# A two-layer graph network in float32: transposing the norms on VectorE with on-chip transfers instead of on TensorE, and the bound check's products made once

## The chip, the cores and the metric

The kernel runs on one core of a Trainium2 chip. A core has TensorE (matrix products and transposes, results in PSUM banks), VectorE, ScalarE, GpSimd and SyncE; SyncE (SP in the profile) issues the transfers, which 16 DMA engines carry out. Each engine works through its own queue in order and waits on semaphores for the others. The metric is the time of one execution in device microseconds, as a median over runs.

## The reference

x holds 64 graphs of 256 nodes with 512 features, adj one 256 x 256 adjacency matrix for all of them. Two layers follow one another; each normalizes x over its features, applies a relu and adds the result of an attention over the neighbours.

```python
def _L0_gnn_ref(X, A, W, a):
    h = jnp.einsum('bnf,fo->bno', X, W)                 # 512 -> 256
    e = h @ a[0] + jnp.swapaxes(h @ a[1], 1, 2)
    e = jax.nn.leaky_relu(e, 0.2) + NEG * (1.0 - A)[None]
    out = jnp.einsum('bij,bjo->bio', jax.nn.softmax(e, axis=-1), h)
    return jnp.concatenate([out, h], axis=-1)

def _L1_gnn_ref(h, adj, Wq, bq, Wk, bk, Wv, bv, Wo, bo):  # 8 heads of 64
    q, k, v = (split_heads(h @ W.T + b) for W, b in ((Wq, bq), (Wk, bk), (Wv, bv)))
    scores = jnp.einsum('bhqd,bhkd->bhqk', q, k) / 8.0
    scores = jnp.where((adj == 0)[None, None], -jnp.inf, scores)
    out = jnp.einsum('bhqk,bhkd->bhqd', jax.nn.softmax(scores, axis=-1), v)
    return out.transpose(0, 2, 1, 3).reshape(b, n, 512) @ Wo.T + bo

h = jnp.maximum(_layernorm(x), 0.0)
x = x + _L0_gnn_ref(h, adj, L0_gnn_W, L0_gnn_a)
h = jnp.maximum(_layernorm(x), 0.0)
x = x + _L1_gnn_ref(h, adj, Wq, bq, Wk, bk, Wv, bv, Wo, bo)
```

The norm of a tile has nodes on its 128 partitions and features along them. A product over the features needs the features on the partitions, so every tile of 128 nodes x 512 features is transposed in both layers.

## The kernel before

**Tiling.** A group is two graphs (`GB = 2`, called batches here), that is four tiles (`GT = 4`) of 128 nodes; there are 32 groups. Everything is float32.

**Stages of a group.** `first_layer(g)` (L396) computes the statistics (`stats`), normalizes and transposes each tile with `norm_T` (L343), multiplies by W (`ph`), forms the neighbour softmax (`pn`, `e`), applies it (`po`), takes the statistics of the new x, normalizes and transposes again into `hT1`, and has GpSimd form sums of quarter blocks of it (`operand_sums`, L374). `project(g)` (L483) makes q, k and v from these by a scheme of seven block products instead of eight (`pq`, `pk`, `pv`; a product numbered 1 to 4 can use a quarter as it stands or one weight sum, those numbered 3, 5, 6 and 7 need `sums`). `scores` (L553) multiplies q and k for four heads (`sc`), ScalarE takes exponentials into `p`, VectorE multiplies by the mask, GpSimd adds halves into `ps`. `weigh` (L581) multiplies by v (`pr`), adds up the denominators (`total`), and VectorE divides into `oT`. `outputs` (L611) makes the output products (`py`), again by seven, from `oT` and GpSimd's `o_sums`; VectorE adds each to x and SP stores it.

**The order.** The generators of three groups are interleaved by a string for each of four steps of an iteration: "u" advances `project(g + 1)`, "o" the outputs, "s" `first_layer(g + 2)`. An iteration ends with the last scores' follow-up, and the next begins with `sc` for group g + 1, at once followed by `pq` for group g + 2 and `py`. TensorE's order is kept as written by `in_order`; a scheduler places the other engines' work. Five PSUM banks go round under the tag `turn` (`mm`), three more are held.

**Norm and transpose.** `normed(t)` subtracts the mean and multiplies by the reciprocal deviation on VectorE into `xn` (two buffers). `put(t, dst)` transposes the four 128 x 128 pieces on TensorE against an identity matrix into a PSUM bank `pt` (L116), and ScalarE's relu takes the bank into `hT`:

```python
pt = mm(f"pt{name}_{t}").rearrange("p (c t) -> p c t", c=HP)
for c in range(HP):
    transpose(pt[:, c, :], xn[t][:, c * P : (c + 1) * P], ident)
nc.scalar.activation(dst, pt, AF.Relu)
```

**The bound check.** `judge()` (L224) bounds scores and values from the weights; if a bound fails, `any_inputs` recomputes everything in another way. It loads blocks of Wq, Wk and Wv again (L247, L267), forms Gram matrices per pair of heads (`gram`), squares them three times (`square`) and adds squares. It runs in places of the main loop where the first layer's generator yields a gap.

**SP's queue.** It holds the loads of x (one per group, L125, into four buffers), the weights' loads, the check's block loads, and one store for each batch (L654). Transfers share eight semaphores in turn, so one waits until the transfer eight places earlier has landed.

Of the kernel before, what the change touches and what calls it, by code (L numbers as in the profile page):

```python
# [8 lines left out]
F32 = mybir.dt.float32  # L9
# [5 lines left out]
P = 128  # L15
# [27 lines left out]
def bounded(  # L43
# [74 lines left out]
    xg = x.rearrange("(g b) (t p) d -> g p (b t) d", b=GB, p=P)  # L118
    og = out.rearrange("(g b) (t p) d -> g p (b t) d", b=GB, p=P)
# [3 lines left out]
    def load(g):  # L123
        xs[g] = big.tile([P, GT, D], F32, tag="x", name=f"x{g}", bufs=4)
        nc.sync.dma_start(xs[g], xg[g])  # L125

    load(0)


# [34 lines left out]

    load(1)
    load(2)


# [40 lines left out]
    def last_bias():  # L209


        pb = mm("pb")
        for q in range(NQ):
            for half in range(2):
                b = small.tile([P, P], F32, tag="power", name=f"bv_{q}_{half}", bufs=1)
                nc.vector.tensor_scalar(b, ones, bv_col[:, half, q : q + 1], None, op0=ALU.mult)
                matmul(
                    pb, b, w_sb["o"][:, half, 2 * q : 2 * q + 2, :],
                    start=(q == 0 and half == 0), stop=(q == NQ - 1 and half == 1),
                )  # L220
        nc.vector.tensor_add(b_out, pb, b_out)


    def judge():  # L224
# [6 lines left out]
        junk = att.tile([P, D], F32, tag="junk", name="junk", bufs=1)  # L231

        def squares(col, *srcs):
            sums = small.tile([P, HP], F32, tag="sums", name=f"sums{col}", bufs=2)
            for i, src in enumerate(srcs):
                nc.scalar.activation(
                    junk[:, : src.free_size()], src, AF.Square, accum_out=sums[:, i : i + 1]
                )
            nc.vector.reduce_sum(part[:, col : col + 1], sums[:, : len(srcs)], axis=AX.X)

        for s in range(2):
            squares(s, w0_sb[:, :, s])
        squares(2, *[w0_sb[:, c, 2:] for c in range(HP)])
        wv = att.tile([P, HP, D // HP], F32, tag="block", name="wv_block", bufs=1)
        sums = small.tile([P, HP], F32, tag="sums", name="sums3", bufs=2)
        for c in range(HP):
            nc.sync.dma_start(  # L247
                wv, wvT[:, c * P : (c + 1) * P].rearrange("(c p) o -> p c o", p=P)
            )
            nc.scalar.activation(  # L250
                junk, wv.rearrange("p c o -> p (c o)"), AF.Square, accum_out=sums[:, c : c + 1]
            )
        nc.vector.reduce_sum(part[:, 3:4], sums, axis=AX.X)
        squares(4, bcol["q"])
        squares(5, bcol["k"])
        squares(6, bv_col.rearrange("p h q -> p (h q)"))
        nc.vector.reduce_max(part[:, 7:8], bad.rearrange("p a t -> p (a t)"), axis=AX.X)
        yield
        heads = const.tile([P, P], F32, name="heads")
        nc.vector.memset(heads, 0.0)  # L260
        for j in range(2):
            nc.vector.memset(heads[j * DH : (j + 1) * DH, j * DH : (j + 1) * DH], 1.0)
        rowsq = const.tile([P, 2, HP], F32, name="rowsq")
        for n, (name, src) in enumerate((("q", wqT), ("k", wkT))):
            for hp in range(HP):
                w = att.tile([P, HP, P], F32, tag="block", name=f"w{name}_block{hp}", bufs=1)
                nc.sync.dma_start(  # L267
                    w, src[:, hp * P : (hp + 1) * P].rearrange("(c p) o -> p c o", p=P)
                )
                yield  # L270
                gram = mm(f"gram_{name}{hp}")[:, :P]
                for c in range(HP):
                    matmul(
                        gram, w[:, c, :], w[:, c, :], start=(c == 0), stop=(c == HP - 1)
                    )
                a = small.tile([P, P], F32, tag="power", name=f"power_{name}{hp}_0", bufs=1)
                nc.vector.tensor_mul(a, gram, heads)
                yield
                for i in range(3):
                    square = mm(f"square_{name}{hp}_{i}")[:, :P]  # L280
                    matmul(square, a, a, start=True, stop=True)
                    if i < 2:
                        a = small.tile(
                            [P, P], F32, tag="power", name=f"power_{name}{hp}_{i + 1}", bufs=1
                        )
                        nc.vector.tensor_copy(a, square)
                    else:
                        nc.scalar.activation(
                            junk[:, :P], square, AF.Square, accum_out=rowsq[:, n, hp : hp + 1]
                        )  # L290
                    yield
        nc.vector.reduce_sum(part[:, 8:10], rowsq, axis=AX.X)
# [45 lines left out]
    def stats(mv, src, t, name):  # L338
        st = small.tile([P, 6], F32, tag="st", name=f"st{name}_{t}")
        nc.vector.bn_stats(st, src[:, t, :])  # L340
        nc.vector.bn_aggr(mv[:, t, :], st)

    def norm_T(src, mv, name):  # L343
# [6 lines left out]
        xn = {}  # L350

        def normed(t):
            xn[t] = att.tile([P, D], F32, tag="xn", name=f"xn{name}_{t}", bufs=2)
            latest[0] = nc.vector.tensor_scalar(  # L354
                xn[t], src[:, t, :], mv[:, t, 0:1], rstd[:, t : t + 1],
                op0=ALU.subtract, op1=ALU.mult,
            ).ins.name

        def put(t, dst):
            if t + 1 < GT:  # L360
                normed(t + 1)
            pt = mm(f"pt{name}_{t}").rearrange("p (c t) -> p c t", c=HP)
            for c in range(HP):
# [710 lines left out]
```

## Time and profile before

| | us |
|---|---|
| three runs | 2698.94, 2701.87, 2702.36 |
| median | 2701.87 |
| the profiled execution | 2699.08 |
| its span, first to last instruction | 2697.3 |
| TensorE busy in that span | 2620.4 |
| VectorE busy | 1669.7 |
| GpSimd busy | 1230.0 |
| ScalarE busy | 835.9 |
| TensorE busy in the first 100 us | 68.4 |
| TensorE busy from 400 to 800 us | 397.3 |
| `pt` products (the transposes), 1024 | 156.2 |
| relu from `pt`, 256 | 153.1 |
| mean granted clock of TensorE | 0.993 |

A line of the profile gives the program's line, the engine, the operation, what is written from what, and the shape. In the groups there follow the total busy time, the mean duration in ns, and the idle time of the engine just before, with what ended it. In a timeline a line begins with the start and the duration in us; "x4" means four instructions one after another, and a number in brackets at the end is idle time before it with its releaser. TensorE's instructions overlap, so the cost of one in a stream is the distance of starts. In a table by stretches there stand, after the bounds and the length, the busy times of TensorE, its weight loads, VectorE, ScalarE and GpSimd, the granted clock, the DMA share and GB/s. "PEclk" in the page is the granted clock in tenths, over 40 slices. A line of the DMA issues ends with KB each and the median us from issue to landing.

### The profile page before, as it was taken

The page shows a single profiled execution, that of the slowest core. Times are in us where ns is not written, and L with a number is a line of the kernel's source. Part 1 is how long each engine was busy: PE and PEld are TensorE (multiplying, and loading weights), DVE is VectorE, ACT ScalarE, POOL GpSimd, SP SyncE. Part 2 cuts the span into 40 slices and gives each one's busy share as a digit, 9 for nine tenths or more (in the row PEclk, how much of TensorE's full clock was granted, in tenths as well). Part 3 has the DMA queues.
Part 4 walks back from the last instruction along what each step waited for, and adds up shares of the span by engine and source line. Part 5 has one row for each costly group of instructions (what it writes and reads, how often), then busy time and mean ns, then how long its engine had stood idle before and what let it go on. Part 6 is the DMA issues. An engine that isn't in the chain of part 4 may idle for free.

```text
span 2697.3 us, 41512 instructions
## 1 busy us (share of the span) xinstructions
PE 2620.4 (97%) x17150; PEld 2118.8 (79%) x17150; DVE 1669.7 (62%) x2558; ACT 835.9 (31%) x1771; POOL 1230.0 (46%) x1004
## 2 busy tenths in 40 slices
PE   5999999999999999999999999999999999999997
PEld 3888888878888887887788888788878878878874
DVE  5666566666557665566665576665576656666544
ACT  2333232333332333323333323333333333233321
POOL 2353355443445443545434454435455335445343
PEclk8999999999999999999999999999999999999998
DMA  5000101000001010000000000000000000000000
GB/s 164 1 12 32 36 24 36 13 32 32 28 32 36 9 36 32 24 32 9 32 32 24 32 32 9 32 32 24 32 32 9 32 32 24 32 17 23 17 16 25
DMA packets 45890, 78.49 MB, mean 29 GB/s; under 512 B 3712, under 2 KB 10624, under 8 KB 45696
## 3 DMA queue, kind: packets, MB, share of 16 engines
q1 hardware_dynamic: 45696, 75.77, 8.1%
q8 instruction: 137, 2.24, 0.3%
q14 instruction: 57, 0.47, 0.1%
HBM read 42.21 MB, written 33.55 MB: 28 GB/s over the span
## 4 chain that ended last, share of the span: by engine, by line
PE 89%; DVE 8%; POOL 1%; issue 1%; DMA 0%; ACT 0%; DVEq 0%
PE pq L113 15%; PE pv L113 14%; PE py L113 13%; PE pk L113 13%; PE pr L113 9%; PE ph L113 8%; PE sc L113 7%; PE po L113 4%; PE pt L116 4%; DVE p L573 3%; DVE r L604 2%; PE total L113 2%; DVE k L544 1%; DVE oT L605 1%; PE pn L116 1%
## 5 line engine op out<-in xcount | busy, mean ns | idle before, releaser
L573 DVE TENSOR_TENSOR p<-p,maskT 128x1024 f32<-128x1024 f32 x256 | 398.6, 1588 | 0.6 <-ACT p L572 0.5
L572 ACT ACTIVATE p<-sc 128x512 f32<-128x512 f32 x512 | 264.4, 602 | 380.9 <-PE sc L113 380.9
L574 POOL TENSOR_TENSOR ps<-p 128x512 f32<-128x512 f32 x256 | 366.2, 1447 | 0.0
L628 DVE TENSOR_TENSOR x<-py,x 128x256 f32<-128x256 f32 x448 | 187.6, 419 | 272.8 <-PE py L113 266.9
L604 DVE RECIPROCAL r<-total 128x256 f32<-128x256 f32 x128 | 224.5, 1754 | 194.6 <-PE total L113 194.6
L113 PE MATMUL py<-wo_sb,o_sums 128*128 128x256 f32 x1024 | 266.5, 384 | 26.4 <-DVE x L628 21.6
L420 POOL TENSOR_TENSOR x<-H,x 128x256 f32<-128x256 f32 x128 | 87.7, 685 | 443.0 <-ACT H L419 441.9
L113 PE MATMUL pr<-p,v 128*32 128x256 f32 x4096 | 251.8, 385 | 5.8 <-DVE p L573 5.8
L113 PE MATMUL sc<-q,k 64*128 64x256 f32 x2048 | 255.7, 389 | 0.0
L113 PE MATMUL pq<-sums,wq_sb 128*128 128x256 f32 x1024 | 246.7, 384 | 4.2 <-POOL sums L377 3.7
L113 PE MATMUL ph<-w_sb,hT 128*128 128x258 f32 x1024 | 246.1, 383 | 0.0
L113 PE MATMUL pk<-sums,wk_sb 128*128 128x256 f32 x1024 | 244.8, 382 | 0.0
L113 PE MATMUL pv<-wv_sb,sums 128*128 128x256 f32 x1024 | 242.0, 379 | 0.1
L113 PEld LDWEIGHTS sc<-q,k 64*128 64x128 f32 x2048 | 187.2, 186 | 69.7 <-issue 52.6
L113 PEld LDWEIGHTS py<-wo_sb,o_sums 128*128 128x128 f32 x1024 | 191.2, 192 | 62.9 <-POOL o_sums L377 37.6
L365 ACT ACTIVATE hT<-pt 128x512 f32<-128x512 f32 x256 | 153.1, 599 | 266.0 <-PE pt L116 265.7
L354 DVE TENSOR_SCALAR xn<-x,mv,rstd 128x512 f32<-128x512 f32 x256 | 225.8, 893 | 9.5 <-PE pt L116 4.9
L376 POOL TENSOR_TENSOR o_sums<-oT 128x256 f32<-128x256 f32 x64 | 106.2, 1660 | 262.6 <-DVE oT L605 262.6
L113 PEld LDWEIGHTS pq<-sums,wq_sb 128*128 128x128 f32 x1024 | 190.1, 191 | 39.1 <-issue 9.9
L113 PEld LDWEIGHTS ph<-w_sb,hT 128*128 128x128 f32 x1024 | 195.7, 192 | 28.6
L113 PEld LDWEIGHTS pk<-sums,wk_sb 128*128 128x128 f32 x1024 | 189.3, 190 | 33.9 <-issue 9.9
L113 PEld LDWEIGHTS pr<-p,v 128*32 128x32 f32 x4096 | 121.1, 110 | 112.2 <-issue 39.7
(145 smaller groups left out, 4054.4 us busy)
## 6 DMA issues: line engine op xcount, KB each, us to landing
x<-in_x_dram SPq DMA_DIRECT2D x32, 1024.0 KB, 5.5
out_dram<-x SPq DMA_DIRECT2D x64, 512.0 KB, 2.8
wq_sb<-in_L_gnn_Wq_dram SPq DMA_DIRECT2D x2, 512.0 KB, 11.7
wk_sb<-in_L_gnn_Wk_dram SPq DMA_DIRECT2D x2, 512.0 KB, 12.4
wv_sb<-in_L_gnn_Wv_dram SPq DMA_DIRECT2D x2, 512.0 KB, 11.4
wo_sb<-in_L_gnn_Wo_dram SPq DMA_DIRECT2D x8, 128.0 KB, 3.3
wv_block<-in_L_gnn_Wv_dram SPq DMA_DIRECT2D x4, 256.0 KB, 3.0
wq_block<-in_L_gnn_Wq_dram SPq DMA_DIRECT2D x4, 256.0 KB, 2.9
```

The costliest lines, as they stand in the source:

```text
L113: in_order(nc.tensor.matmul(*args, **kwargs))
L116: in_order(nc.tensor.transpose(*args))
L354: latest[0] = nc.vector.tensor_scalar(xn[t], src[:, t, :], mv[:, t, 0:1], rstd[:, t : t + 1], op0=ALU.subtract, op1=ALU.mult,).ins.name
L365: nc.scalar.activation(dst, pt, AF.Relu)
L376: nc.gpsimd.tensor_add(sums[:, 0], a21, a22)
L420: nc.gpsimd.tensor_add(xt[:, t, F1:], H[:, t, 2 : F1 + 2], xt[:, t, F1:])
L544: nc.vector.tensor_add(part(1, 1), first, p7)
L572: nc.scalar.activation(pair[:, j], sc[j], AF.Exp, scale=scale)
L573: nc.vector.tensor_mul(pair, pair, maskT[:, None, :, :].to_broadcast([P, 2, NT, N]))
L574: nc.gpsimd.tensor_add(ps[:, 2 * i : 2 * i + 2, :], pair[:, :, 0, :], pair[:, :, 1, :])
L604: nc.vector.reciprocal(r, total)
L628: nc.vector.tensor_add(to, out, to)
```

## The change

Except in group 0, a tile's norm is no longer transposed on TensorE. VectorE transposes it in 32 x 32 blocks into `xt`; 16 transfers per batch, each 32 partitions x 2 tiles with runs of 512 bytes, move the blocks between partition groups into `moved`; ScalarE's relu reads `moved` in the order that `hT` needs. The work of a batch is split: `norm` for its two tiles, `turn` (transposes and transfers), and later `placed` (the two relus), with a yield between them. The loads of x are one per batch (seven buffers). The check takes its products from the weights already on the chip, for all four pairs of heads of a matrix in one bank, and is advanced while group 0's first layer and projection run; its block loads are gone. `last_bias` makes its columns on GpSimd into one wide tile. The three `kept` tiles of `project` share one tag with two buffers.

```diff
-    def load(g):
-        xs[g] = big.tile([P, GT, D], F32, tag="x", name=f"x{g}", bufs=4)
-        nc.sync.dma_start(xs[g], xg[g])
+    def load(g, b):
+        xs[g, b] = big.tile([P, NT, D], F32, tag="x", name=f"x{g}_{b}", bufs=7)
+        nc.sync.dma_start(xs[g, b], xg[g, b])
...
+        b = att.tile([P, 2, 2, P], F32, tag="kept", name="bv_wide")
         for q in range(NQ):
             for half in range(2):
-                b = small.tile([P, P], F32, tag="power", name=f"bv_{q}_{half}", bufs=1)
-                nc.vector.tensor_scalar(b, ones, bv_col[:, half, q : q + 1], None, op0=ALU.mult)
+                nc.gpsimd.tensor_scalar(
+                    b[:, half, q, :], ones, bv_col[:, half, q : q + 1], None, op0=ALU.mult
+                )
...
+        for n, name in enumerate(("q", "k")):
+            gram = bank(f"gram_{name}")
+            for hp in range(HP):
+                half, cols = hp // 2, slice(hp % 2 * P, (hp % 2 + 1) * P)
+                for c in range(HP):
+                    w = w_sb[name][:, c % 2, c // 2 * 2 + half, cols]
+                    matmul(gram[:, hp, :], w, w, start=(c == 0), stop=(c == HP - 1))
+            power[name] = room[:, n * HP : (n + 1) * HP, :]
+            nc.vector.tensor_mul(
+                power[name], gram, heads[:, None, :].to_broadcast([P, HP, P])
+            )
+            yield
+        for i in range(3):
+            for n, name in enumerate(("q", "k")):
+                square = bank(f"square_{name}{i}")
+                for hp in range(HP):
+                    a = power[name][:, hp, :]
+                    matmul(square[:, hp, :], a, a, start=True, stop=True)
...
+                yield
...
-    def norm_T(src, mv, name):
+    def norm_T(src, mv, name, by_pe):
...
+        def turn(b):
+            tiles = range(b * NT, (b + 1) * NT)
+            if by_pe:
+                for t in tiles:
+                    turned[t] = mm(f"pt{name}_{t}").rearrange("p (c n) -> p c n", c=HP)
+                    for c in range(HP):
+                        transpose(turned[t][:, c, :], xn[t][:, c * P : (c + 1) * P], ident)
+                return
+
+            J = P // S
+            xt = att.tile([P, J, NT, P], F32, tag="xt", name=f"xt{name}_{b}")
+            moved = att.tile([P, NT, J, P], F32, tag="moved", name=f"moved{name}_{b}")
+            for t in tiles:
+                nc.vector.transpose(
+                    xt[:, :, t % NT, :].rearrange("p j (n c) -> p j c n", c=HP),
+                    xn[t].rearrange("p (c j a) -> p j c a", j=J, a=S),
+                )
+                turned[t] = moved[:, t % NT].rearrange("p i (n c) -> p c (i n)", c=HP)
+            for i in range(J):
+                for j in range(J):
+                    nc.sync.dma_start(
+                        moved[j * S : (j + 1) * S, :, i, :], xt[i * S : (i + 1) * S, j]
+                    )
+
         def put(t, dst):
...
+            nc.scalar.activation(dst, turned[t], AF.Relu)
...
-        put = norm_T(xt, mv, f"1_{g}")
+        norm, turn, put = norm_T(xt, mv, f"1_{g}", by_pe)
+        norm(0)
+        norm(1)
         yield GAP
         hT = big.tile([P, HP, TOK], F32, tag="hT1", name=f"hT1_{g}")
-        for t in range(GT):
-            put(t, hT[:, :, t * P : (t + 1) * P])
-            if t == GT - 1:
-                break
-            yield
+        ahead((turn, 0), (norm, 2), (norm, 3))
+        yield GAP
+        ahead((turn, 1))
+        yield GAP
+        placed(0, hT[:, :, :N])
+        yield GAP
+        placed(1, hT[:, :, N:])
...
-                s = att.tile([P, 2, N], F32, tag=f"kept{i}", name=f"kept{i}_{name}_{g}", bufs=1)
+                s = att.tile([P, 2, N], F32, tag="kept", name=f"kept{i}_{name}_{g}")
...
-    gaps = 0
-    for part in first_layer(0):
-        gaps += part is GAP
-        if part is GAP and gaps == 3:
+    verdict = judge()
+    for piece, _ in enumerate(first_layer(0)):
+        if piece == 8:
+            next(verdict)
+        if piece == 13:
             last_bias()
+            next(verdict)
+        if piece == 15:
             weight_sums("q")
     short = first_layer(1) if NG > 1 else none
     for i, _ in enumerate(project(0)):
-        if i % 7 == 1:
+        if i in (1, 8, 15):
             weight_sums("kvo"[i // 7])
         next(short, None)
+        next(verdict, None)
+    run(verdict)
     run(short)
-    verdict = judge()
...
-            if step == 1 and g + 3 < NG:
-                load(g + 3)
+            if step % 2 and g + 3 < NG:
+                load(g + 3, b)
...
-                elif next(short, GAP) is GAP:
-                    next(verdict, None)
+                else:
+                    next(short, None)
```

The first layer's norm is split in the same way, with `turn` and `placed` for each batch, before the `ph` products; the second batch's relus stand after the second `ph`. Elsewhere `xt[:, r, ...]` becomes a list of tiles `xt[r]` with the same operations.

## The prediction

> **What bounds the kernel now.** I read the busy shares first, then the costly groups, then the timeline of one iteration of the main loop, the DMA issues and the clock by stretches.
>
> ```profile
> PE 2620.4 (97%) x17150; PEld 2118.8 (79%) x17150; DVE 1669.7 (62%) x2558; ACT 835.9 (31%) x1771; POOL 1230.0 (46%) x1004
> ...
> PEclk8999999999999999999999999999999999999998
> ...
> L365 ACT ACTIVATE hT<-pt 128x512 f32<-128x512 f32 x256 | 153.1, 599 | 266.0 <-PE pt L116 265.7
> L354 DVE TENSOR_SCALAR xn<-x,mv,rstd 128x512 f32<-128x512 f32 x256 | 225.8, 893 | 9.5 <-PE pt L116 4.9
> ```
>
> TensorE is busy 97% at full clock, so what leaves it shortens the run, as long as nothing else becomes late. What a transpose costs on TensorE is read from starts, not from busy time:
>
> ```profile
> 1659.64 0.60 PE L116 MATMUL pt<-ident,xn 128*128 128x128 f32 x4
> 1659.84 0.59 ACT L514 COPY kept_v<-pv 128x512 f32<-128x512 f32 x1 [2.87 <-PE pv L113]
> 1659.97 1.60 PEld L113 LDWEIGHTS pv<-wv_sb,sums 128*128 128x128 f32 x8
> 1660.08 1.89 PE L113 MATMUL pv<-wv_sb,sums 128*128 128x256 f32 x8
> ```
>
> Four transposes start at 1659.64 and the next product at 1660.08; over several such places the step is 0.43 us a tile. In the same iteration GpSimd turns the transposed norms into operands:
>
> ```profile
> 1668.66 1.28 POOL L376 TENSOR_TENSOR sums<-hT 128x512 f32<-128x512 f32 x1 [1.22 <-PE pv L113]
> ...
> 1670.73 2.00 PE L113 MATMUL sc<-q,k 64*128 64x256 f32 x16
> ...
> 1675.50 1.59 POOL L377 TENSOR_TENSOR o_sums<-o_sums,oT 128x256 f32<-128x256 f32 x1
> ...
> 1677.95 1.03 PE L113 MATMUL py<-wo_sb,o_sums 128*128 128x256 f32 x4
> ```
>
> GpSimd's chain (three `sums`, the fourth, two `o_sums`) runs from 1668.66 to 1677.1, 8.4 us, and TensorE takes the result at 1677.95, 7.2 us after the scores (`sc`) begin. That chain has 0.85 us to spare today.
>
> **The change, part by part.**
>
> 1. *Transposes leave TensorE.* 31 of 32 groups x 8 tiles = 248 x 0.433 = 107.4 us off.
>
> 2. *The bound check leaves the main loop.* On the chain of waits one iteration's first scores stand at 191.31 and, twelve iterations on, at 1176.49: 82.10 us each. The next takes 86.58 (to 1263.07), later ones 81.55 (to 1344.62). The excess is 12 x 0.55 + 5.0 = 11.6 us; the products stand ahead of the loop instead, and 12 block loads (L247, L267) leave SP's queue.
>
> 3. *The start.* TensorE is busy 68.4 of the first 100 us. `pb` no longer passes through one buffer (its four steps lie between 45.40 and 52.8), and its columns are made by GpSimd: the first `pq` can start near 46.5 instead of 55.91, -9. The six squaring steps of four products add 6 x 0.87 = 5.2 between the products of `project(0)`. Group 1's own moves are exposed: its second layer has only seven `pv` products and one `sc` (14 us) over a path of about 31 us (the steps of part 4), some 17 us, of which the shorter products ahead give back a few. I take +5 for the whole start, with bounds of -9 and +20.
>
> 4. *The new path* is two block transposes on VectorE per batch (T each), 16 DMAs of 32 KB on SP's queue, and two relus on ScalarE. I follow it where it is tightest: the second layer of group g+2, at the end of an iteration. Zero is the start of its last `po` product (in the trace: 1649.17). TensorE then has `pk`, `py`, `pr`, `total`, `sc`, seven `pv`, `pr`, `total`, and reaches the next iteration's `sc` at +22.3 by its steps (1.73 a product, 0.87 a `py`, 1.75, 0.55, 1.93); the `py` that needs `o_sums` is due 7.2 later, at +29.5.
>    Supply: VectorE has the last statistics and `ve` at +3.9 (reciprocal starts 1.07 after `po`; 0.17, 0.48, 0.69 and the next group's first statistics in front), GpSimd's power takes 1.2, two `xn` unblocked 0.54 each: +6.2. T is not in the trace. At the same tile of 128x512 f32 the nearest rows are `xn` 0.54 and a tensor-tensor 0.69; the slowest VectorE row is the reciprocal, 1.75. I take 0.69: +7.6.
>    SP: the nearest rows have the same shape, 32 partitions x 2 runs, back to back:
>
> ```profile
> 24.57 0.42 SPq L187 DMA_DIRECT2D bv_col<-in_L_gnn_bv_dram  x1
> 25.04 0.43 SPq L186 DMA_DIRECT2D wo_sb<-in_L_gnn_Wo_dram  x1
> 25.51 0.42 SPq L187 DMA_DIRECT2D bv_col<-in_L_gnn_bv_dram  x1
> ...
> bv_col<-in_L_gnn_bv_dram SPq DMA_DIRECT2D x8, 0.2 KB, 2.4
> bq_sb<-in_L_gnn_bq_dram SPq DMA_DIRECT2D x1, 2.0 KB, 2.2
> ```
>
>    0.47 us from issue to issue and 2.3 to landing. Bounds: 0.31 (the isolated issues from 15.10 on) and 1.36 (their spacing while earlier transfers are waited for) for the one, 0.31 (no landing before the issue is over) and 5.5 (the 1 MB load) for the other. The first batch's 16, with the x load between them (0.5), hold SP to +15.6. The second batch's blocks are ready by then (a reciprocal 1.75, two `xn`, `oT` 0.69, two `p` products at 1.22, two T: +14.9; with mean durations +16.4). Its last DMA is issued at +22.65 and lands at +24.95; two relus, 1.2: +26.15; GpSimd's 8.4 us: +34.6. Due at +29.5, so TensorE stands still for 5.1 us.
>    Queued behind: ScalarE's relu waits for 16 DMAs, and the exponentials of the next scores stand behind it, then VectorE's `p` products and the `x` addition that empties the bank of `py`. That path comes to about +30.6, inside the same stall. On SP the next group's 32 DMAs follow; their `ph` is not due before about +43, and they land by +33.4 and +40.9. Stores and loads of x stand in the gaps between the bursts.
>    A stall of this length also lowers the clock:
>
> ```profile
> 104.00:108.00 4.00, 2.25 (x13) 2.00 (x14) 3.09 (x5) 0.80 (x2) 2.98 (x3) 1.00 0.00 0
> ...
> 1254.00:1258.00 4.00, 3.25 (x10) 2.79 (x11) 2.31 (x6) 0.60 (x1) 2.92 (x2) 0.57 0.00 0
> ...
> 1254.74 1.12 PE L116 MATMUL pt<-ident,xn 128*128 128x128 f32 x4 [2.92 <-DVE xn L354]
> 1255.65 2.95 PE L113 MATMUL pv<-wv_sb,hT 128*128 128x256 f32 x8
> ```
>
>    After 2.17 us of idleness at 105.75 the granted clock stays 1.00; after 2.92 us it is 0.57 in the next 4 us, the transposes take 0.91 instead of 0.43 and the product 2.79 instead of 1.73: +1.5.
>    So 5.1 + 1.5 = 6.6 us for each of the 30 iterations that prepare a later group: +198.
>    The loads of x by halves I put at nothing: they are issued 40 us and more ahead of use (without that cover, the 5.5 us to landing of a load). So too the three `kept` buffers that become two: the third product's copy waits for the first one's addition (0.68), which lies behind two products of 1.73; uncovered it would be 3 x 0.68 = 2 us an iteration.
>
> **Sum against the profiled execution.** 2697.3 - 107.4 - 11.6 + 5 = 2583.3 without stalls; + 198 = 2781.3 of span. That execution took 2699.08, 1.8 more than its span, and the median of the runs is 2.8 above it: 2786.
>
> **Two rules of the skill that speak against it.** T by the rows is 0.69. The Trainium skill ("VectorE: DVE Perf Modes", The three transpose paths) says that VectorE transposes only within 32x32 blocks and that a full 128x128 transpose belongs on TensorE. It gives 311 ns for a 128x128 bf16 tile; as an estimate from that page four make 1.24 us for T, the second batch's blocks would come at about +17.1, and the sum would be about 45 us higher. For the transfers the rows above give 0.47 us each, overlapped. The skill ("DMA: Bandwidth & Descriptors", Bandwidth) calls transfers under 64 KB dominated by their descriptors and lists 0.68 us at 4 KB and 0.95 at 64 KB; as an estimate from that page, 16 transfers of 0.8 one after another would take 12.8 us instead of 7.5, the second batch would land about 10 us later, and the sum would be about 300 us higher.
>
> **Rivals.**
> - *A, the forecast: the move path is too long by 5 us an iteration.* For it: the 8.4 us chain with 0.85 to spare, and 32 issues in a row on one queue. Against it: issue and landing between on-chip buffers are in no row.
> - *B, issues are quick.* At 0.31 us an issue the second batch starts with VectorE at +14.9 and lands at +21.85: a stall of 2.0 with no loss of clock, 60 us in all: 2583.3 + 60 + 4.6 = 2648. Faster. It decides below 3.8 us an iteration ((2697.3 - 2583.3) / 30), that is, when the second batch lands before about +23.7 (+22.2 with the loss of clock).
> - *C, all is hidden.* Landing by +19.9 needs issues under 0.2 us: 2583.3 + 4.6 = 2588. For it only that no row excludes it.
> - *D, VectorE is late too.* T of 1.4 and mean durations put the second batch's blocks at +19.2: a stall of 8.7 + 1.5, 306 us: 2894. For it: the four-dimensional patterns of the transpose and VectorE's share of 62%, which 248 x T raises; against it: the `xn` and tensor-tensor rows.
>
> **Chances.** A 0.62, B 0.15, C 0.10, D 0.08; 0.05 for an outcome so near 3.8 us an iteration that it is no change (within 0.2%, which is what a measurement of this kernel can tell). Faster 0.25, same 0.05, slower 0.70. A's own range is 2710 to 2855 (1.0 us either way in issues, landing and T moves the sum by 30). The range for 8 in 10 reaches down through B: 2620 to 2855.
>
> **What would show it.** In the new profile: `pt` groups only in group 0; an iteration of about 78.1 us plus the stall, 84 to 85 in all; TensorE waiting once an iteration at the `py` product for GpSimd's `o_sums`, which waits for the relu, which waits for the `moved` DMAs; granted clock of 0.5 to 0.7 just after; 16 DMAs at 0.47 us and T near 0.69; no check products after 115 us. Landings before +22, or issues of 0.3 us, would make the forecast wrong, and iterations near 78 us would show it.

## The result, and the profile after

The changed kernel takes 3034.62 us (median; 3032.71 to 3036.09) against 2700.94 us for the kernel before on the same chip: a ratio of 1.1236, 95% interval 1.1216 to 1.1255. The forecast was slower, 2786 us; it is slower by 334 us instead of 84, above the forecast's range of 2620 to 2855.

The page of the profile after, head, clock by slices, two groups and one transfer line:

```profile
PE 2664.0 (88%) x16158; PEld 2085.9 (69%) x16158; DVE 1829.0 (60%) x2783; ACT 950.7 (31%) x1759; POOL 1231.1 (41%) x1008
...
PEclk9899999999999999999999999999999999999998
...
L382 ACT ACTIVATE hT<-moved 128x512 f32<-128x512 f32 x248 | 266.6, 1125 | 349.9 <-DMA moved<-xt 349.7
...
L370 DVE STREAM_TRANSPOSE xt<-xn 128x512 f32<-128x512 f32 x248 | 257.5, 1095 | 39.0 <-DMA moved<-xt 39.0
...
moved<-xt SPq DMA_DIRECT2D x1984, 32.0 KB, 1.9
```

TensorE has 992 instructions fewer, which are the 248 x 4 transposes, yet it is busy for 2664 us instead of 2620 and idle for 367 instead of 77. Its mean granted clock is 0.941 instead of 0.993. The relu takes 1.125 us and the block transpose 1.095.

The waits of TensorE in the kernel after (us in total, times, longest):

```profile
PE py L113 <- POOL o_sums L389: 144.6, 31, 5.0
...
PE pv L113 <- ACT kept_v L551: 78.6, 30, 4.7
```

One end of an iteration in the kernel after, in the order of the new path (the timeline, start and duration in us). Its wait at `py` is one of the two shortest; most are near 5.0 us, as the list of waits says (144.6 us in 31 times):

```profile
1670.62 1.03 PE L113 MATMUL po<-H,e 128*128 128x257 f32 x4
...
1675.63 1.00 DVE L352 TENSOR_SCALAR xn<-x,mv,rstd 128x512 f32<-128x512 f32 x2 [0.74 <-POOL rstd L347]
...
1676.55 2.07 DVE L370 STREAM_TRANSPOSE xt<-xn 128x512 f32<-128x512 f32 x2
...
1678.68 2.18 SPq L377 DMA_DIRECT2D moved<-xt  x3
...
1680.96 0.53 SPq L125 DMA_DIRECT2D x<-in_x_dram  x1
...
1689.87 3.11 PE L113 MATMUL pv<-wv_sb,hT 128*128 128x256 f32 x8 [2.58 <-ACT kept_v L551]
...
1694.84 3.78 PE L113 MATMUL pv<-wv_sb,sums 128*128 128x256 f32 x8 [1.86 <-DVE v L581]
...
1701.70 2.14 ACT L382 ACTIVATE hT<-moved 128x512 f32<-128x512 f32 x2 [2.45 <-DMA moved<-xt]
...
1703.91 1.27 POOL L388 TENSOR_TENSOR sums<-hT 128x512 f32<-128x512 f32 x1 [12.59 <-ACT hT L382]
...
1711.49 0.72 POOL L389 TENSOR_TENSOR o_sums<-o_sums,oT 128x256 f32<-128x256 f32 x1
...
1712.26 1.13 PE L113 MATMUL py<-wo_sb,o_sums 128*128 128x256 f32 x4 [2.94 <-POOL o_sums L389]
```

From the start of the last `po` to the `py` that needs `o_sums` it is 41.64 us; the forecast had 34.6. SP's queue in the same stretch:

```profile
1681.54 39.61 SPq L377 DMA_DIRECT2D moved<-xt  x61
```

61 issues in a row without a gap, 0.65 us each. The first 32 (with the three before the load) are this group's second layer, the other 32 the next group's first layer.

Over the starts of `pv` of some twenty iterations (between 600 and 2410 us), the mean iteration of the kernel after is 91.98 us (81.96 before) and the mean distance from `po` to `py` 42.11 (29.17 before).

### The profile page after: what moved, and what is told of

Read it like the earlier page. It is cut to its first block, busy times and chain, and to the rows that moved or that the text cites. A ratio compares the mean times of both kernels' runs of the same rounds, so it can differ in the third digit from the quotient of the medians.

```text
span 3031.1 us, 42733 instructions
## 1 busy us (share of the span) xinstructions
PE 2664.0 (88%) x16158; PEld 2085.9 (69%) x16158; DVE 1829.0 (60%) x2783; ACT 950.7 (31%) x1759; POOL 1231.1 (41%) x1008
## 4 chain that ended last, share of the span: by engine, by line
PE 66%; POOL 9%; DVE 9%; SPq 8%; issue 3%; ACT 3%; DMA 3%; DVEq 0%; ACTq 0%; POOLq 0%
PE pk L113 13%; PE py L113 12%; PE pq L113 11%; SPq L377 7%; PE ph L113 7%; PE pr L113 7%; PE sc L113 7%; PE po L113 4%; PE pv L113 3%; DVE p L610 3%; POOL sums L389 2%; DVE xt L370 2%; POOL sums L390 2%; DMA moved<-xt 2%; PE total L113 2%
## 5 line engine op out<-in xcount | busy, mean ns | idle before, releaser
L610 DVE TENSOR_TENSOR p<-p,maskT 128x1024 f32<-128x1024 f32 x256 | 429.0, 1707 | 14.0 <-ACT p L609 13.8
L113 PE MATMUL py<-wo_sb,o_sums 128*128 128x256 f32 x1024 | 291.7, 417 | 148.0 <-POOL o_sums L389 144.6
L382 ACT ACTIVATE hT<-moved 128x512 f32<-128x512 f32 x248 | 266.6, 1125 | 349.9 <-DMA moved<-xt 349.7
L113 PE MATMUL pv<-wv_sb,hT 128*128 128x256 f32 x768 | 228.2, 458 | 78.6 <-ACT kept_v L551 78.6
L113 PE MATMUL pq<-sums,wq_sb 128*128 128x256 f32 x1024 | 284.3, 428 | 12.9 <-POOL sums L389 10.3
L370 DVE STREAM_TRANSPOSE xt<-xn 128x512 f32<-128x512 f32 x248 | 257.5, 1095 | 39.0 <-DMA moved<-xt 39.0
L113 PEld LDWEIGHTS pq<-sums,wq_sb 128*128 128x128 f32 x1024 | 222.8, 220 | 63.2 <-POOL sums L389 12.9
L113 PEld LDWEIGHTS pv<-wv_sb,sums 128*128 128x128 f32 x1024 | 196.3, 194 | 93.7 <-DVE v L581 67.2
L113 PEld LDWEIGHTS pv<-wv_sb,hT 128*128 128x128 f32 x768 | 167.9, 225 | 128.0 <-ACT kept_v L551 90.6
L113 PEld LDWEIGHTS sc<-q,k 64*128 64x128 f32 x2048 | 187.8, 187 | 70.6 <-issue 53.3
L507 POOL TENSOR_TENSOR x<-x,b_out 128x512 f32<-128x512 f32 x128 | 199.1, 1565 | 76.2 <-DVE xn L352 71.7
```

Source lines behind the costliest of these rows:

```text
L113: in_order(nc.tensor.matmul(*args, **kwargs))
L370: nc.vector.transpose(xt[:, :, t % NT, :].rearrange("p j (n c) -> p j c n", c=HP), xn[t].rearrange("p (c j a) -> p j c a", j=J, a=S),)
L382: nc.scalar.activation(dst, turned[t], AF.Relu)
L507: nc.gpsimd.tensor_add(xt[t], xt[t], b_out)
L610: nc.vector.tensor_mul(pair, pair, maskT[:, None, :, :].to_broadcast([P, 2, NT, N]))
```

## The experiments

Twelve kernels were run. "Path" is the mean distance from the last `po` to the first `py` that reads `o_sums`, "iteration" the mean distance of `pv` starts, both read from the timelines.

| run | us | ratio to before, 95% | iteration | path |
|---|---|---|---|---|
| all_pe | 2748.86 | 1.0187 (1.0170 to 1.0204) | 83.19 | 32.43 |
| layout | 2973.76 | 1.1017 (1.0998 to 1.1035) | 89.84 | 40.26 |
| four | 2839.52 | 1.0521 (1.0504 to 1.0539) | 86.36 | 38.65 |
| free_kept | 3000.08 | 1.1117 (1.1099 to 1.1136) | 90.58 | 41.94 |
| one_run | 2954.34 | 1.0936 (1.0917 to 1.0954) | 89.18 | 39.74 |
| two_q | 2806.10 | 1.0391 (1.0374 to 1.0408) | 84.59 | 36.91 |
| layout_four_free | 2805.65 | 1.0397 (1.0379 to 1.0414) | 85.17 | 37.60 |
| hybrid_free | 2765.54 | 1.0253 (1.0236 to 1.0271) | 83.81 | 35.60 |
| pe_tiles | 2695.93 | 0.9983 (0.9974 to 0.9993) | 81.54 | 28.76 |
| hybrid3 | 2669.58 | 0.9886 (0.9870 to 0.9903) | 80.61 | 29.47 |
| rev | 3123.61 | 1.1569 (1.1550 to 1.1588) | 95.21 | 34.88 |
| full | 2958.66 | 1.0956 (1.0937 to 1.0974) | 90.23 | 38.83 |

In `rev` the first thing late is a `pq` product instead of `py`, so its path column is not comparable.

### Without the moves: all_pe and pe_tiles

The line that selects, as `pe_tiles` has it (in both runs the relu follows each tile's transposes at once; the restaging is not shown):

```diff
-        by_pe = g == 0
+        by_pe = [True, True]
```

> The transposes of both layers are TensorE's again in every group (relu straight from PSUM); the check's products, the loads by halves and the two kept buffers stay as in the changed kernel. Theory M (the loss comes from the move path alone: blocks, 32 issues on one queue, landing, relus, GpSimd's chain): 2697 - 11.6 + 5 = about 2690 us, no wait at pv for kept_v. Rival K (the two kept buffers, where there were three, cost on their own what the pv waits show, 2.6 + 1.9 us an iteration): 2690 + 30 x 4.5 = about 2825 us.

> Both layers go by TensorE tile by tile in the steps of the kernel before (the run all_pe turned two tiles in one step, and its relus for the second half of hT0 stood on ScalarE's queue ahead of work that they wait for); the check's products ahead of the loop, the loads by halves and two kept buffers stay as in the changed kernel. Theory M (those three parts cost next to nothing where nothing is late): 2697 - 11.6 + some 11 for the start, as all_pe's first scores show (126.4 instead of 114.9 us) = 2697 us, 2685 to 2705. Rival P (the two kept buffers or the loads by halves cost by themselves): 2740 to 2750 us.

`all_pe` came out at 2749, between its two theories. Its `kept_v` wait is gone, so rival K does not explain it. Its timeline shows two waits in each iteration that the kernel before does not have:

```profile
1526.65 1.11 PE L116 MATMUL pt<-ident,xn 128*128 128x128 f32 x8 [1.49 <-DVE xn L352]
...
1559.64 1.62 PE L113 MATMUL sc<-q,k 64*128 64x256 f32 x8 [0.74 <-ACT p L612]
```

Two tiles are turned in one step, so the second pair waits for norms that VectorE reaches late; and ScalarE's exponentials are late. That is the experiment's own way of staging. `pe_tiles` turns tile by tile as before: the waits at `pt` come to 13.5 us in all instead of 36.2, those at `sc` (22.2) are gone, and it takes 2695.93, as theory M said (2697). The check ahead of the loop, the loads by halves and the two `kept` buffers together therefore cost nothing that stays, and they gain 0.17% (interval 0.07 to 0.26%). The whole 339 us between `pe_tiles` and the changed kernel belong to the moves and their staging.

### Where the path is: rev

```diff
-        by_pe = g == 0
+        by_pe = [True, g == 0]
```

> The reverse of the hybrid: the first layer's tiles go by TensorE tile by tile, the second layer's by VectorE's blocks and the transfers (order of the run named layout), two kept buffers. Theory M (the whole loss sits in the second layer's path, some 40 us from the last po to py): the path stays, half the transfers and blocks of the iteration are gone for nothing and TensorE has its 54 us of first-layer transposes again, partly inside its wait: 2960 to 3030 us. Rival L (the loss goes by how much is moved, and the queue or VectorE are simply too full): half of it, (2974 + 2696) / 2 = about 2835 us.

Half the moves are gone, and the kernel is slower still, 3124 us: above the range of M and far from rival L. The load of the queue is not the reason; the second layer's path is. TensorE in `rev`:

```profile
1566.60 3.78 PE L113 MATMUL pq<-sums,wq_sb 128*128 128x256 f32 x8 [4.49 <-POOL sums L394]
```

The last `po` started at 1525.77, so this product waits until 40.8 us after it, with the same chain behind it, and it runs at half its usual speed (3.78 us instead of 1.89). Of the 146 us of span over `layout`, TensorE's idle time makes 75.8 (400.1 us against 324.3) and its busy time 70.6; of the busy time the first layer's transposes are 31 x 4 x 0.433 = 54. So the path was the one that theory M named, and its price was too low.

### The sizes on the path: layout, one_run, four

```diff
-                    xt[:, :, t % NT, :].rearrange("p j (n c) -> p j c n", c=HP),
+                    xt[:, :, t % NT, :].rearrange("p j (c n) -> p j c n", c=HP),
...
-                turned[t] = moved[:, t % NT].rearrange("p i (n c) -> p c (i n)", c=HP)
+                turned[t] = moved[:, t % NT].rearrange("p i (c n) -> p c i n", c=HP)
```

> The element order inside a 512-byte run becomes (c n) instead of (n c): VectorE writes and ScalarE reads runs of 32 elements instead of elements 16 bytes apart; the transfers keep their shape and number. Theory M with a stride as the cause of the long instructions: the block transpose falls from 1.10 to about 0.7 us and the relu from 1.12 to about 0.6; 2 x 0.4 + 2 x 0.52 = 1.9 us of the path an iteration, 30 x 1.9 = 56 us, about 2979 us. Rival N (the operations take 1.10 and 1.12 us whatever the order): 3034 us.

The groups of `layout`:

```profile
L370 DVE STREAM_TRANSPOSE xt<-xn 128x512 f32<-128x512 f32 x248 | 163.8, 687 | 31.7 <-DMA moved<-xt 29.9 <-issue 1.1 <-DVE xn L352 0.3
...
L384 ACT ACTIVATE hT<-moved 128x512 f32<-128x512 f32 x248 | 142.5, 622 | 411.9 <-DMA moved<-xt 411.0 <-issue 0.4 <-ACT H L450 0.2
```

Both sizes fall, 1.095 to 0.687 and 1.125 to 0.622 us, by the order of elements alone; the path falls by 1.85 us and the time to 2973.76. The expectation was 1.9 and 2979. So the prediction's 0.69 for a block and 0.6 for a relu would have been right for a pattern of 32 neighbouring elements, and the change has one with elements 16 bytes apart.

`one_run` lays the two tiles of a batch side by side (`moved` as `[P, J, NT, P]`): one run of 1 KB a partition.

> As the run named layout, and moved is laid out so that the two tiles of a batch lie next to each other in it: a transfer of 32 partitions has one run of 1 KB a partition instead of two of 512 bytes; 16 transfers a batch as before. Theory M with issues whose time goes by the runs: an issue falls from 0.645 to about 0.5 us, 32 x 0.15 = 4.6 us of the path an iteration, 2974 - 138 = about 2836 us. Rival F (an issue has a fixed price whatever its runs): 2974 us within 10.

2954.34: neither 2836 nor 2974 within 10, but clearly on the side of rival F. Its transfers on SP, by duration (min, median, max in ns):

```profile
L377 SPq DMA_DIRECT2D moved<-xt x1984: 507/589/2053, 66.9 to 2815.3; - x199
```

In the kernel after the same row has 585/595/1923. With half the runs the shortest issue falls from 0.585 to 0.507 us, the usual one hardly. The 20 us are an iteration shorter by 0.66 us, 0.5 of it in the path; part of that is the landing, 1.8 us instead of 1.9.

```diff
-                for j in range(J):
-                    nc.sync.dma_start(
-                        moved[j * S : (j + 1) * S, :, i, :], xt[i * S : (i + 1) * S, j]
-                    )
+                nc.sync.dma_start(moved[:, :, i, :], xt[:, i])
```

> A batch is moved by 4 transfers of 128 partitions instead of 16 of 32, the same bytes in the same 512-byte runs; the order of the 32 by 32 blocks inside hT is then not the reference's. Theory M (the number of issues on SP's queue is the largest term): 4 x 0.6 instead of 16 x 0.645 us a batch, the second batch lands at +21 to +23 instead of +31 after the last po product, TensorE's wait falls to 2 to 4 us plus 1.5 of clock: 2690 to 2755 us. Rival R (the transfers' time goes by their runs and bytes, not by their number): landing as late as now, 3030 us.

Four times the bytes per transfer, and an issue has nearly the same price (durations as above):

```profile
L376 SPq DMA_DIRECT2D moved<-xt x496: 593/614/2031, 68.6 to 2698.4; - x166
```

and the waits of TensorE:

```profile
PE pv L113 <- DVE v L578: 105.3, 30, 4.7
...
PE pv L113 <- ACT kept_v L548: 77.1, 31, 4.1
```

So the number of issues sets the price, and with a quarter of them 195 us go: the iteration is 5.6 us shorter, 3.5 of it in the path and 2.1 behind it, where the granted clock now stays at 1.00. But 2840 is above M's 2690 to 2755: the wait at `py` for GpSimd is gone, and TensorE waits 6.0 us an iteration at `pv` where VectorE's `v` additions stand behind the blocks and ScalarE's copies behind the relu that waits for the landing.

### The next limits: free_kept, layout_four_free, two_q

```diff
-            p1 = kept(first, 0, 0)
+            take(part(0, 0), first, 0)
...
-            latest[0] = nc.vector.tensor_add(part(0, 0), second, p1).ins.name
+            latest[0] = nc.vector.tensor_add(part(0, 0), second, part(0, 0)).ins.name
```

> The first product of each projection is copied straight into its part of the result and added to there, so that two kept buffers serve the two products that are left and none waits. Theory M (the pv waits lie between the last po and py, where the move path of 41.6 us sets the end anyway; they are absorbed): the kept_v wait at pv goes, the wait at py grows by as much, 3034 us within 10 (a little less if the clock dips only once). Rival K (the pv waits add to the iteration): 30 x 2.6 to 4.4 us less, 2900 to 2955 us.

The `kept_v` wait disappears, and the next one in the same place takes it over:

```profile
PE pv L113 <- DVE v L581: 173.2, 30, 6.0
...
PE py L113 <- POOL o_sums L389: 113.1, 32, 5.0
```

The path stays (41.94 against 42.11). The waits at `pv` lie on TensorE's side of a path whose other side is longer, as M said; the time fell by 34 us all the same, three times M's tolerance. It lies outside the path (the iteration is 1.40 us shorter, the path 0.17), in the clock: of 27 iterations (last `po` between 250 and 2700 us) 15 have a lowered clock in the 4 us after the wait at `py`, in the kernel after 25. Without a lowered clock an iteration takes 47.8 us outside the path in both. M had allowed for the clock without giving it a number.

> The runs named layout, four and free_kept together (4 transfers of 128 partitions a batch; the order of the blocks inside hT is not the reference's). In four, TensorE waited 6.0 us an iteration at pv, for VectorE's v additions (3.5, behind the blocks in VectorE's order) and for ScalarE's kept_v copy (2.5, behind the relu that waits for the landing). Theory V (VectorE's order is the next limit): eight blocks an iteration that are 0.4 us shorter take 2 to 3 us of that wait away: 2840 - 75 = about 2765 us, less (2720) if the shorter path spares the clock too. Rival W (only the landings set these waits): 2820 to 2840 us.

2805.65, between the two theories: V had the direction (34 us), at less than half the size, and how much of it the first product's place gives was not separated. The `kept_v` wait fell to 16.9 us in all, while the wait for `v` rose to 135.6: VectorE does blocks, norms, statistics and the softmax's products in that stretch. That its order is what decides was not tried by itself.

```diff
-                    nc.sync.dma_start(
+                    (nc.sync if j % 2 else nc.scalar).dma_start(
```

> As the runs named layout and free_kept together, and every second transfer of a batch is issued on ScalarE's queue instead of SP's. Theory M (issues in a row on one queue are the largest term): two queues issue a batch in half the time, the second batch lands some 10 us earlier, the path from the last po to py falls from 41.6 to about 30 us, TensorE's wait at py goes; ScalarE's own work stands behind its issues, so some wait at pv stays: 2700 to 2850 us. Rival G (the transfers themselves are the limit, or ScalarE's copies behind the issues cost as much): 2920 to 2960 us.

2806.10, within M, though the path fell only to 36.91 us and not to about 30. The wait at `py` for GpSimd is gone, and the time is 168 us below `layout`; the first product's place, worth 34 us in `free_kept`, is in it. An issue costs as much on either queue (medians 601 ns on SP, 607 on ScalarE), and the two run at the same time. The price is a wait for ScalarE's copy, which stands among its issues (TensorE's waits):

```profile
PE pv L113 <- ACT v L553: 90.2, 30, 4.0
```

### Which layer can move: hybrid_free, hybrid3, full

> The first layer's tiles go by VectorE and the transfers, in the order of the run named layout, the second layer's by TensorE; the first product is copied straight into its part of the result. Theory M (only the second layer's move path is on the end; the first layer's is due some 20 us later): TensorE loses 31 x 4 x 0.433 = 54 us of transposes against all_pe and gains no wait: 2749 - 54 = about 2695 us. Rival X (the first layer's blocks and the relus that wait for landings stand ahead of VectorE's and ScalarE's work for the products in any case): 2750 to 2800 us.

2765.54: rival X. Against `all_pe` 54 us of TensorE's work are gone, and the time is 17 us longer. ScalarE and VectorE in one place of it:

```profile
1551.65 1.15 ACT L387 ACTIVATE hT<-moved 128x512 f32<-128x512 f32 x2 [3.04 <-DMA moved<-xt]
...
1552.71 1.06 ACT L614 ACTIVATE p<-sc 128x512 f32<-128x512 f32 x2
...
1553.81 1.23 DVE L615 TENSOR_TENSOR p<-p,maskT 128x1024 f32<-128x1024 f32 x1 [3.42 <-ACT p L614]
...
1555.52 1.10 PE L113 MATMUL py<-wo_sb,o_sums 128*128 128x256 f32 x4 [1.84 <-DVE x L672]
```

A relu stands on ScalarE's queue for 3.04 us until its transfers land; behind it wait two exponentials, behind these VectorE's product, then its addition to x, then TensorE. Nothing of this is the first layer's own due time. `hybrid3` changes the order only, in three places. The diff shows the blocks and the relus; the third turns the second layer's tiles one by one, as `pe_tiles` does:

```diff
+                if last["v"]:
+                    after(block, last["v"])
...
+            if last["copy"]:
+                after(relu, last["copy"])
...
             ahead((turn, 1))
             yield GAP
+            yield GAP
             placed(0, hT[0])
```

> As hybrid_free (first layer by VectorE and transfers, second by TensorE), with three changes of order alone: the second layer tile by tile as in the kernel before, the first layer's blocks behind the last v addition on VectorE, its relus one step later and behind the copies of the q products on ScalarE. Theory Q (hybrid_free's waits, 33 us at pt, 26 at pv, 56 at py, come from what stands in front on VectorE and ScalarE): most of these 115 us go: 2643 to 2690 us, below the kernel before. Rival X (VectorE has no room for the blocks wherever they stand): the waits reappear elsewhere, 2720 to 2765 us.

2669.58, ratio 0.9886: theory Q, and a version faster than both kernels. The three changes were not tried one by one. Of `hybrid_free`'s 115 us of waits, the 33.0 at `pt` are for norms and have nothing to do with a transfer (5.2 here); the 25.9 at `pv` are gone, and the 56.0 at `py` are 42.0. Its waits of TensorE that recur, and SP in one iteration:

```profile
PE py L113 <- DVE x L694: 26.6, 31, 1.0
PE py L113 <- POOL o_sums L400: 15.4, 31, 2.1
```

```profile
1568.40 22.54 SPq L382 DMA_DIRECT2D moved<-xt  x32
```

The 32 issues still take 22.5 us, and ScalarE's relus wait 12.5 us for them in the whole run instead of 98: here nobody needs them earlier. Against `pe_tiles` the moves of one layer (with the first product in its place, as in `free_kept`) are worth 26 us of the 54.

> Both layers by VectorE and transfers in all groups but the first, in the order of the run named layout, with hybrid3's changes of order for the first layer, the first product copied straight into its part of the result, and every second transfer of the second layer issued on GpSimd's queue. Theory M (two queues halve the second layer's issues): the path falls from 41.6 to about 30 us as in two_q, and ScalarE's copies no longer stand behind issues: 2620 to 2720 us. Rival Z (an issue on GpSimd takes its time from the sums, or over 1 us each): 2780 to 2900 us.

2958.66, above both theories. GpSimd takes 0.54 us an issue and does nothing else meanwhile:

```profile
1553.11 8.51 POOL L382 DMA_DIRECT2D moved<-xt  x16
...
1564.09 1.04 POOL L347 TENSOR_TENSOR rstd<-ve,rexp 128x4 f32<-128x4 f32 x1
...
1565.17 1.96 DVE L352 TENSOR_SCALAR xn<-x,mv,rstd 128x512 f32<-128x512 f32 x2 [6.61 <-POOL rstd L347]
```

The next group's power (`rstd`) stands behind the issues, VectorE waits 6.61 us for it, and then its reciprocal is late, for which TensorE waits 3.69 us. That is rival Z's mechanism (GpSimd's own time), on other work than the sums that it named and at a higher price.

## Why the prediction was wrong

*Transposes off TensorE, check out of the loop.* Right. 992 instructions are gone, and `pe_tiles` has the sum 2697.3 - 11.6 + 6 = 2692 for a measured span of 2693.9.

*The start, +5.* In `pe_tiles`, without the moves, it is +6.1 (the second iteration's first scores at 197.38 instead of 191.24). In the changed kernel the first scores stand at 133.07 instead of 114.88: +18.2, inside the bounds of -9 and +20, but 13 more than taken. The first iteration then takes 95.8 us (76.4 before; the terms of the prediction make 79.5). Start and first iteration together cost 29 us more than the sum had.

*The path from the last `po`.* The mechanism is the one named: blocks, 32 issues on one queue, landing, relus, GpSimd's 8.4 us, and TensorE waiting at `py` for `o_sums` (4.7 us on average, 5.1 predicted, after it has already lost time at `pv` inside the path). Of its sizes, in the iteration shown:

| term | prediction | measured | on the path |
|---|---|---|---|
| norms ready | +6.2 | +5.9 | -0.3 |
| block transposes of the first batch | 2 x 0.69 | 2.07 | +0.7 |
| 32 issues | 0.47 each | 0.65 each | +5.7 |
| landing | 2.3 | 1.9 | -0.4 |
| two relus | 1.2 | 2.14 | +0.9 |
| GpSimd's chain | 8.4 | 8.3 | 0 |
| last `po` to `py` | 34.6 | 41.6 | +7.0 |

The table's parts come to 6.6; the x load (0.58 for 0.5) and gaps between steps are the rest. The step that failed is "0.47 us from issue to issue". The rows that it was taken from had the same 32 partitions and 0.2 KB in turn with 128 KB, all from HBM; `one_run` and `four` show that neither runs nor bytes make the difference. An on-chip source alone does not make it either. The stores of x read from the chip too (duration: min, median, max in ns, kernel after):

```profile
L692 SPq DMA_DIRECT2D out_dram<-x x64: 372/384/522, 203.2 to 3025.6; - x64
```

A load of x from HBM takes 0.37 us by itself (at 1634.59) and 0.53 among the moves, a store 0.38 and 0.52 just behind them, a move never under 0.585. Whether it is both ends on the chip or the pattern of the transfer stays open. The bounds written down were 0.31 to 1.36, but the range let issues, landing and T move by 1.0 us together: 32 issues multiply an error of 0.18 by 32, and the range had no such factor.

*T at 0.69 and the relu at 0.6.* Both were read from rows of the same shape, with other patterns. The diff's `(n c)` said that elements go 16 bytes apart; the relu's price was not even given bounds. `layout` prices both together at 61 us.

*The second batch's blocks hidden behind the first batch's issues.* Right: they are done at 1688.0 (+17.4; mean durations gave +16.4), and SP reaches them at about 1689.8. So rival D, VectorE late too, did not decide here; it did as soon as the issues were fewer (`four`).

*Queued behind, "inside the same stall".* Right for the changed kernel, but not harmless in itself: in `hybrid_free` the chain that the same relu begins, followed in one place, ends at `py`, where TensorE waits 56.0 us in all for VectorE's x (0.8 in `all_pe`).

*The `kept` buffers at nothing.* Without the moves right (`pe_tiles`); with them uncovered, 2.6 us an iteration at `pv`, close to the 2 us given for it. It lies inside the path; what came back without it, 34 us (`free_kept`), came mostly through the clock.

*The loss of clock, 1.5 us after `py`.* Right in kind and place, and too small. Of the 27 iterations of the kernel after whose last `po` lies between 250 and 2700 us, 25 wait 3.53 to 5.03 us at `py`, have a granted clock of 0.50 to 0.57 in the 4 us that follow, and take 50.0 us from `py` to the next last `po`. The two others, the one shown above among them, wait 3.08 and 2.94 us, keep 1.00 and take 47.8. So the loss is 2.2 us. The rest is 0.8 shorter than the prediction's 78.1 - 29.5 = 48.6, and the mean, 49.9, comes out near its 50.1 by these two errors against each other. A usual case:

```profile
1801.86 2.07 PE L113 MATMUL py<-wo_sb,o_sums 128*128 128x256 f32 x4 [5.01 <-POOL o_sums L389]
1803.73 3.34 PE L113 MATMUL pq<-sums,wq_sb 128*128 128x256 f32 x8
```

Why 2.94 us cost nothing and the 2.58 us at `pv` did can be read from the trace. In all fourteen traces the changes of the granted clock lie on a grid of 3.41 us. Stretches of this grid in the kernel after (bounds, length, busy times of the five engines' rows, granted clock, DMA share, GB/s):

```profile
1687.19:1690.60 3.41, 0.83 (x4) 0.68 (x4) 2.98 (x8) 0.58 (x1) 1.50 (x2) 1.00 0.25 55
1690.60:1694.01 3.41, 2.38 (x6) 1.35 (x4) 2.65 (x4) 2.14 (x2) 0.73 (x1) 0.50 0.23 51
...
1707.67:1711.08 3.41, 1.65 (x8) 1.12 (x6) 3.32 (x4) 0.00 (x0) 3.41 (x3) 1.00 0.23 49
1711.08:1714.49 3.41, 2.23 (x10) 1.99 (x11) 0.42 (x1) 2.17 (x2) 3.33 (x5) 1.00 0.27 60
```

The wait of 2.58 us lies within one stretch, TensorE is busy for 0.83 us of it, and the next stretch has half the clock. The boundary at 1711.08 divides the wait of 2.94 us into 1.76 and 1.18, and the clock stays. The two waits that the prediction read in the kernel before fit: the 2.92 us leave 2.55 of one stretch idle, the 2.17 us are divided at 104.09.

*The sum.* 29 iterations x (91.98 - 84.7) = 211 (the mean path is 7.5 us longer than the prediction's 34.6, the rest 0.2 shorter), and 29 for the start and the first iteration: 2781.3 + 240 = 3021 of the measured span of 3031.1. Some 10 us are not assigned.

*The two rules of the Trainium skill.* Both spoke in the right direction for the second layer. "DMA: Bandwidth & Descriptors", Bandwidth, calls transfers under 64 KB dominated by their descriptors; measured, an issue of 32 KB costs 0.595 us and one of 128 KB 0.614, so the bytes indeed do not set the price, but half as many runs (0.589) do not lower it either; the estimate of 0.8 us from that page (its figures are the transfers' own time for loads from HBM issued by GpSimd, not the time of an issue) was 0.15 too high, 0.47 from the rows 0.18 too low. "VectorE: DVE Perf Modes", Rules for kernel authors, sends a 128x128 transpose to TensorE; measured, a 128x512 tile takes 1.095 us on VectorE (0.687 with the other order) against 0.433 on TensorE, and the 32 transfers behind it hold SP for 21 us, so the rule holds for the layer on the path. For the first layer `hybrid3` gains 26 us against it.

*The rivals.* B (2648) and C (2588) would have needed issues of 0.31 us and less; the shortest issue of a move in the trace is 0.585.

## What to carry to other kernels

Before work leaves the busiest engine, add up the new path in time from its last input to its first user, and multiply every doubtful unit price by its count before the range is set: 32 issues in series weigh more than all else that was estimated. Move what is due late, not what is due next: the same transposes gain 1.0% (26 us) in the layer that has time to spare and cost 9 to 16% with the one that has none, as long as its 32 issues stand on one queue. An instruction that waits for a transfer holds everything behind it on its engine, so its place in that engine's order is part of the price; three changes of order, of which this was one, were worth 96 us together (`hybrid_free` to `hybrid3`).

## What the runs showed of the hardware

- An issue of an on-chip transfer on SP's queue costs about 0.6 us for each size tried: 595 ns for 32 KB in 512-byte runs, 589 in 1 KB runs, 614 for 128 KB over 128 partitions; in a row they follow at 0.65. A store of 512 KB from the chip to HBM on the same queue costs 0.384 (all medians). Two queues issue side by side at the same price each. On GpSimd it is 0.54 us of that engine's own time.
- The order of elements inside a tile makes an instruction of the same shape 1.6 to 1.8 times as long: block transpose 1.095 and 0.687 us, relu 1.125 and 0.622.
- The granted clock changes only on a grid of 3.41 us, and TensorE's idle time within one stretch of the grid (its length less the busy time of products) tells the next stretch's clock. In the fourteen traces, from 150 us to 200 us before the end, a stretch at full clock was followed by full clock with up to 2.00 us idle and by half with 1.88 us or more; a stretch at half clock was followed by full clock with up to 0.57 us idle and by half with 0.60 us or more. So the same wait costs nothing or several us, by where it falls.
